# Full-height matrix products, no one-column products, and another placing of the preparation in a fused graph and state-space kernel

## The chip, the cores and the metric

The kernel runs on one core of a Trainium2 chip. The metric is the device time in microseconds of one execution. The engines are named as in the profile: PE (matrix products), DVE (vector), ACT (activations), POOL (GpSimd) and SP (which issues most DMAs).

## The reference

The input is x with shape (16, 96, 64, 64), float32. Two layers are computed. The first is a graph convolution on windows of 8x8 pixels; the second is a Mamba block with two inner layers on the sequence of 4096 pixels, followed by a fusion product and a batch norm. Cut to what matters:

```
# graph layer, per window of 64 nodes with 96 channels
y    = fc1(x)                                  # 1x1 convolution, scale, shift
xn   = nodes / max(norm(nodes), 1e-12)
idx  = top_k(-(sq - 2 xn xn^T + sq^T), 9)      # the 9 nearest nodes, itself among them
h    = gelu(ew [x_i ; x_j - x_i])              # 192 channels, for each neighbour j
x1   = fc2(max over j of h) + x
# Mamba block, twice, per sequence of 4096 pixels
h    = layernorm(seq) * ln_g + ln_b
xs,z = split(h @ in_w)                         # 192 channels each
xc   = silu(causal conv of 4 taps of xs)
dt,B,C = split(xc @ xproj_w)                   # 6, 16 and 16 columns
delta  = softplus(dt @ dt_w + dt_b)
s_t  = exp(delta A) s_(t-1) + delta B xc       # 192 channels x 16 states
y    = sum over states of s C + D xc
seq += (y * silu(z)) @ out_w
# end
out  = batchnorm(fus_w [seq ; relu(mean(x1) @ gp_w^T)]) + x1
```

## The kernel before

The sequence of an image is cut into 8 chunks of 512 pixels (one row of windows each). An item n = (b, i, k) is chunk k of inner layer i of image b; there are 16x2x8 = 256 items. An item has 8 slots p, one for each pair of the 16 states, so the main loop (L741) has 2048 slots. Channels and the two states of a pair lie on the 128 partitions, as three blocks c of 512 columns.

A slot does the following. DVE makes two products db (L648) of u = delta xc with bt and then three scans (L789); the first db of the next slot comes between the second and the third scan. bt is the row of B broadcast to the partitions by a PE product with the selecting matrix bsel (L643); it has one PSUM buffer, so PE makes the next bt when DVE has made the last db of the present one, and DVE needs it ahead of its third scan. ACT computes the decays da (L637) two slots ahead (`AHEAD`). POOL multiplies the states hb with the broadcast C, ct (L803). PE folds the two halves of the product of the slot before into ya and yb (L659, L661), and at p = 3 adds D xc with a diagonal matrix (L656, L657). At p = 1 of the next item DVE gates y with z (L667).

All other work is written as Python generators. In each slot, ahead of the second scan (`c == 1`), every generator in the list `going` is advanced by one step up to its next `yield`. So the order on each engine is written out by hand: a step's instructions stand in each engine's queue between those of the slot. The main ones, with the slot in which each starts:

- `norm` (L509), started at p = 7 for item n+3: the centred product pc (L520), its square on ACT (L522), and the sum over channels by `by_pixel` (L271): four products whose weights are 96x128 pieces of the square and whose moving operand is the one column ones_c, giving the variances as 128x4. DVE scales them (L527), POOL takes the power -0.5 (L530), and two DMAs through DRAM spread it over the 96 partitions (rs, L533 and L535). POOL makes hn (L538).
- `prelude` (L540), started at p = 5 for item n+2 at the head of the list: the convolution and z products (L555, L560) with SiLU on ACT (L567), the product pd (L579), its copy dbl (L584), the products pdta and pdtb (L593, L596) and the softplus as four ACT passes (L600 to L607), four POOL passes (L609 to L613), and 12 DMAs that arrange delta and u.
- `nearest` (L288) and `edges` (L360), one row of windows in two items: fc1, norms of the nodes (again by `by_pixel`, ss, with POOL powers and DMAs), similarities sc, top 8 on DVE; then one-hots on ACT (L384, L385), products pv, gathered products t (L404, L407) with GELU on ACT (L412), maxima over the neighbours on DVE (L793, one after each scan, out of the queue `between`), the maximum against the own node sa (L455), and the product pf with fc2 (L462, L465), added to x on DVE (L474).
- `tail` (L670), started at p = 4: the product with out_w, added to seq on DVE (L686), and in the second inner layer the fusion product po (L693), o on ACT (L695) and statistics on DVE (L697).

Two mechanisms matter. Products of steps use the PSUM pool `ps_m` (pm) in turn, which has two buffers: a product waits until the one two before it has been read. And `apart` splits a step: its product is made at the end of the present slot's steps, and DVE's use of it stands at the head of the next slot's. ACT's exponential and SiLU or GELU lie in different tables; a step that yields `TABLE` keeps `ahead` from running in the next slot, so that the table changes once.

The products of bt, pdta and pdtb contract over 39 rows (6 + 32 columns of pd and a row of ones), those of the convolution and z over 97 (96 channels and a row of ones).

Before the loop, the first image's 8 rows of windows and the first items are prepared by `drain`; behind it the batch norm streams all outputs from DRAM.

```
    for m, (n, p) in enumerate(order):
        ...
        if p == 7 and n + 3 < NI:
            going.insert(0, norm(n + 3))
        if p == 5 and n + 2 < NI:
            going.insert(0, prelude(n + 2))
        ct, das = soon.pop((n, p))
        dbs = [first, times_b(n, p, 1, bt), times_b(n, p, 2, bt)]
        if after is not None:
            bt = bcast(*after)
        if p == 0 and behind is not None:
            folded(*behind, y)
```

## Time and profile before

| | |
|---|---|
| median of 3 runs | 14862.89 us (14855.65 to 14863.29) |
| profiled execution, its own time | 14897.12 us |
| its span | 14895.3 us |
| mean granted TensorE clock | 0.891 |
| PE busy | 13574.3 us (91%) |
| DVE busy | 13114.8 us (88%) |
| ACT busy | 10114.4 us (68%) |
| POOL busy | 10278.8 us (69%) |
| scans L789, with carried state | 5376 of 1269 ns mean |
| db L648 | 6144 of 680 ns mean |
| POOL hb L803 | 2048 of 3450 ns mean |
| ACT da L637 | 6144 of 710 ns mean |

The mean of an instruction includes its start and end phases, which overlap with its neighbours'; where times are added up along an engine, the distance from start to start is the right measure (1.19 us for a scan, 0.59 us for a db in DVE's timeline). A float32 product has two records on PE for each instruction. An engine's busy share is a mean over the whole span; which engine a slot waits for is read from the waits and from windows of the timeline.

### The profile page before, as it was taken

What the parts mean: (1) busy time and instruction counts of PE and PEld (TensorE: products, weight loads), DVE (VectorE), ACT (ScalarE), POOL (GpSimd) and SP (SyncE); (2) the same over time, 40 slices, a digit from 0 to 9 for tenths busy, and PEclk for the clock granted to TensorE, in tenths of its full rate; (3) what the DMA queues carried; (4) which work ended last, traced back from release to release, by engine and by line L of the source; (5) the groups of instructions that cost most, each with busy time, mean ns of one, the idle gap of its engine ahead of it and who ended that gap; (6) DMA issues with size and microseconds to landing.
All of it is one profiled execution on the core that took longest, in us unless ns stands there. A gap on an engine that the chain in (4) does not pass through costs nothing. (4 is left out here: it accounts for less than half of the span.)

```text
span 14895.3 us, 168323 instructions
## 1 busy us (share of the span) xinstructions
PE 13574.3 (91%) x50248; PEld 5491.6 (37%) x50248; DVE 13114.8 (88%) x17401; ACT 10114.4 (68%) x14517; POOL 10278.8 (69%) x6279
## 2 busy tenths in 40 slices
PE   5799999999999999999999999999999999999982
PEld 2233333333333333333333333333333333333330
DVE  2699999999998999999999999999999999999984
ACT  4477777777777777777777777777777677677652
POOL 0577777777777777777777777777777777777771
PEclk8799899989998999999999999999999999989885
DMA  1233333333333333333333333333333333333337
GB/s 27 61 82 86 83 82 83 84 83 81 86 84 79 85 84 83 80 85 85 81 84 84 83 81 86 84 80 85 83 83 82 84 86 80 85 83 82 81 81 218
DMA packets 934023, 1256.95 MB, mean 84 GB/s; under 512 B 304672, under 2 KB 436142, under 8 KB 923888
## 3 DMA queue, kind: packets, MB, share of 16 engines
q1 hardware_dynamic: 929520, 1221.01, 31.7%
q10 hardware_dynamic: 3584, 25.17, 0.4%
q8 instruction: 396, 6.49, 0.2%
q14 instruction: 523, 4.28, 0.1%
HBM read 756.89 MB, written 85.98 MB: 57 GB/s over the span
## 5 line engine op out<-in xcount | busy, mean ns | idle before, releaser
L803 POOL TENSOR_TENSOR hb<-hb,ct 128x1536 f32<-128x1536 f32 x2048 | 7065.1, 3450 | 678.1 <-DVE hb L789 187.2
L789 DVE TENSOR_TENSOR_SCAN hb<-da,state,db 128x512 f32<-128x512 f32 x5376 | 6781.1, 1269 | 0.0
L648 DVE TENSOR_TENSOR db<-u,bt 128x512 f32<-128x512 f32 x6144 | 3992.1, 680 | 672.4 <-PE bt L643 670.3
L637 ACT ACTIVATE da<-delta,a 128x512 f32<-128x512 f32 x6144 | 3900.5, 710 | 61.6 <-DVE hb L789 48.6
L643 PE MATMUL bt<-dbl,bsel 39*128 39x512 f32 x4096 | 2466.0, 683 | 333.6 <-DVE db L648 330.3
L659 PE MATMUL ya<-hb,fold 128*64 128x512 f32 x8192 | 2424.8, 673 | 89.4 <-POOL hb L803 89.1
L802 POOL COPY state<-hb 128x3 f32<-128x3 f32 x1792 | 337.8, 189 | 2975.2 <-DVE hb L789 2550.8
L412 ACT ACTIVATE g<-t,eb,es 128x512 f32<-128x512 f32 x1536 | 1184.8, 777 | 1015.8 <-PE t L404 728.1
L567 ACT ACTIVATE xc<-pj,conv_b 128x512 f32<-128x512 f32 (+1 forms) x512 | 297.4, 581 | 1959.6 <-PE pj L555 1018.8
L661 PE MATMUL yb<-hb,fold 128*64 128x256 f32 x8192 | 1368.8, 415 | 0.0
L404 PE MATMUL t<-oh,vu 128*128 128x512 f32 x2048 | 1176.1, 700 | 45.7 <-ACT vu L393 29.4
L661 PEld LDWEIGHTS yb<-hb,fold 128*64 128x64 f32 x8192 | 640.5, 150 | 1359.0 <-issue 1358.7
L643 PEld LDWEIGHTS bt<-dbl,bsel 39*128 39x128 f32 x4096 | 659.4, 201 | 1164.1 <-DVE db L648 634.7
L555 PE MATMUL pj<-hn,conv_in 97*128 97x512 f32 x2048 | 953.0, 608 | 27.9 <-POOL hn L538 27.9
L789 DVE TENSOR_TENSOR_SCAN hb<-da,db 128x512 f32<-128x512 f32 x768 | 922.6, 1209 | 0.0
L659 PEld LDWEIGHTS ya<-hb,fold 128*64 128x64 f32 x8192 | 503.6, 145 | 1070.4 <-issue 726.9
L407 PE MATMUL t<-oh,vu 128*64 128x512 f32 x2048 | 583.7, 649 | 214.2 <-ACT g L412 209.2
L584 ACT COPY dbl<-pd 38x512 f32<-38x512 f32 x256 | 148.3, 579 | 855.9 <-PE pd L581 855.9
L404 PEld LDWEIGHTS t<-oh,vu 128*128 128x128 f32 x2048 | 386.2, 211 | 801.4 <-issue 521.4
L793 DVE TENSOR_REDUCE hqa<-g 128x64 f32<-128x512 f32 x960 | 634.1, 661 | 0.4 <-ACT g L412 0.3
L390 PE MATMUL pv<-ewT,y 96*64 96x192 f32 x2048 | 478.1, 361 | 124.7 <-ACT sqv L522 124.4
L384 ACT ACTIVATE oh<-idb,minus_node 64x1024 f32<-64x1024 uint16 x512 | 586.9, 1146 | 6.7 <-DMA idb<-idxd 6.7
(160 smaller groups left out, 18671.8 us busy)
## 6 DMA issues: line engine op xcount, KB each, us to landing
ct<-cd SPq DMA_DIRECT2D x4096, 128.0 KB, 3.0
delta<-ln SPq DMA_DIRECT2D x1024, 128.0 KB, 2.4
u<-s SPq DMA_DIRECT2D x1024, 128.0 KB, 2.3
idb<-idxd SPq DMA_DIRECT2D x256, 256.0 KB, 4.0
delta<-ln SPq DMA_DIRECT2D x1024, 64.0 KB, 2.0
u<-s SPq DMA_DIRECT2D x1024, 64.0 KB, 2.0
rs<-rsd SPq DMA_DIRECT2D x256, 192.0 KB, 3.4
x<-in_x SPq DMA_DIRECT2D x128, 192.0 KB, 4.5
```

What stands on the lines that cost most here:

```text
L384: nc.scalar.activation(ohj, idb[:, 2 * p : 2 * p + 2, :], AF.Abs, bias=minus_node)
L404: nc.tensor.matmul(t, lhsT=vus[p][:, part, :128], rhs=ohw[part], start=True, stop=True)
L412: nc.scalar.activation(g, t, AF.Gelu, bias=e_b[:, j : j + 1], scale=e_s[:, j : j + 1])
L555: nc.tensor.matmul(ps, lhsT=wt[:, t, :128], rhs=hn[:, off : off + Q], start=(t == 0), stop=(t == taps - 1))
L637: nc.scalar.activation(da, delta[:, c, :], AF.Exp, scale=a_neg[i][:, c, p : p + 1])
L643: nc.tensor.matmul(bt, lhsT=bsel[:, p, :], rhs=made[n][2], start=True, stop=True)
L648: nc.vector.tensor_tensor(db, made[n][5][:, c, :], bt, ALU.mult)
L659: nc.tensor.matmul(y[0][half(h)], lhsT=fold, rhs=hb[:, h, :], start=(p == 0), stop=(p == NPR - 1))
L661: nc.tensor.matmul(y[1][half(h)], lhsT=fold, rhs=hb[:, 2, bass.ts(h, QH)], start=(p == 0), stop=(p == NPR - 1))
L789: nc.vector.tensor_tensor_scan(hb[:, c, :], das[c], dbs[c], state[:, p, c : c + 1] if k else 0.0, ALU.mult, ALU.add)
L793: between.popleft()()
L803: nc.gpsimd.tensor_tensor(hb, hb, ct.unsqueeze(1).to_broadcast([128, NB3, Q]), ALU.mult)
```

## The change

It has these parts.

- The one-column products go. The sums over channels are made by one product with a 96x96 matrix of ones (ones_cc), which gives the sum on all 96 partitions at once. For `norm` ACT takes Ln and Exp(-0.5 ·) of it, and the DVE and POOL steps and both DMAs go. For `nearest` ACT copies one row, which two DMAs through DRAM arrange as 128x4; the clamp moves to POOL.
- bsel, hn, dbl, z_in, conv_in and dt_w get 128 rows; the added weight rows are zero and the added rows of hn and dbl are ones.
- `norm` starts at p = 0 for item n+2, `prelude` at p = 4 at the end of the list, with one `yield` fewer ahead of pd and one more ahead of the exponentials; `tail` starts at p = 6, `pooled` at k = 5.
- The one-hots of both halves are made in one step, right after the wait for their indices, instead of in the steps of pv.
- The maxima over neighbours are queued a slot later (`later` has two stages), and the maximum against sa goes after the second scan of its slot (`late`).
- The decays are computed ahead at p = 2 and 4 (`BURSTS`) and at the end of the slots.
- D xc is added at p = 0 instead of p = 3. z has four buffers, o shares the buffer of xn, and hqa and hqb are allocated later.

```diff
-    bsel = const.tile([R + 2 * NS + 1, NPR, 128], F32, name="bsel")
+    bsel = const.tile([128, NPR, 128], F32, name="bsel")
...
-        t = const.tile([R + 2 * NS + 1, Q], F32, name=f"dbl{i}")
+        t = const.tile([128, Q], F32, name=f"dbl{i}")
...
-            wc = const.tile([C + 1, NT, D], F32, name=f"conv_in{i}")
+            wc = const.tile([128, NT, D], F32, name=f"conv_in{i}")
+            nc.vector.memset(wc, 0.0)
...
+        ss = pm.tile([C, Q], F32, tag="mm", name=f"ss_{nm}")
+        nc.tensor.matmul(ss, lhsT=ones_cc, rhs=sq, start=True, stop=True)
+        nc.scalar.copy(sq[0:1], ss[0:1])
+        ss_d = dram.tile([1, Q], F32, tag="ss_d", name=f"ssd_{nm}")
+        nc.sync.dma_start(out=ss_d, in_=sq[0:1])
         r4 = pr.tile([128, 2, QJ], F32, tag="r4", name=f"r4_{nm}")
-        apart(partial(by_pixel, sq, f"ss_{nm}"), clamped)
+        nc.sync.dma_start(out=r4[:, 1], in_=ss_d.rearrange("o (p j) -> (o p) j", j=QJ))
+        yield
+        yield
+        nc.gpsimd.tensor_scalar(r4[:, 0], r4[:, 1], 1e-24, None, ALU.max)
...
             yield
+            for p in range(2):
+                ohj = ohs[p][0:NN].rearrange("j w i k -> j w (i k)")
+                nc.scalar.activation(ohj, idb[:, 2 * p : 2 * p + 2, :], AF.Abs, bias=minus_node)
+                nc.scalar.activation(ohj, ohj, AF.Relu, bias=1.0, scale=-1.0)
             yield
...
-                    later.append(
+                    later[1].append(
...
+        late.append(partial(nc.vector.tensor_tensor, hqa, hqa, sa, ALU.max))
+        late.append(partial(nc.vector.tensor_tensor, hqb, hqb, sb, ALU.max))
...
-        v4 = pr.tile([128, QJ], F32, tag="v4", name=f"v4_{nm}")
-        apart(
-            partial(by_pixel, sq, f"pvar_{nm}"),
-            lambda ps: nc.vector.tensor_scalar(v4, ps, 1.0 / C, EPS, ALU.mult, ALU.add),
-        )
-        yield
-        nc.gpsimd.tensor_tensor(v4, v4, mhalf, ALU.pow)
-        yield
-        rs_d = dram.tile([128, QJ], F32, tag="rs_d", name=f"rsd_{nm}")
-        nc.sync.dma_start(out=rs_d, in_=v4)
+        ps = pm.tile([C, Q], F32, tag="mm", name=f"pvar_{nm}")
+        nc.tensor.matmul(ps, lhsT=ones_cc, rhs=sq, start=True, stop=True)
         rs = pr.tile([C, Q], F32, tag="rs", name=f"rs_{nm}")
-        nc.sync.dma_start(out=rs, in_=rs_d.rearrange("p j -> (p j)").unsqueeze(0).to_broadcast([C, Q]))
-        yield
+        nc.scalar.activation(rs, ps, AF.Ln, bias=eps_t[:C], scale=1.0 / C)
+        nc.scalar.activation(rs, rs, AF.Exp, scale=-0.5)
         yield
...
-        if p == 7 and n + 3 < NI:
-            going.insert(0, norm(n + 3))
-        if p == 5 and n + 2 < NI:
-            going.insert(0, prelude(n + 2))
+        if p == 0 and n + 2 < NI:
+            going.insert(0, norm(n + 2))
+        if p == 4 and n + 2 < NI:
+            going.append(prelude(n + 2))
...
-                if p == 4 and n:
+                if p == 6 and n:
                     going.append(tail(n - 1))
                 open_steps()
-                if not held:
+                if p in BURSTS:
                     ahead()
...
+            while c == 1 and late:
+                late.pop(0)()
```

## Prediction

> **What bounds the kernel now.** I read the page first, then the waits, the stretches by window and the timeline of one period. The page:

> ```profile
> span 14895.3 us, 168323 instructions
> PE 13574.3 (91%) x50248; PEld 5491.6 (37%) x50248; DVE 13114.8 (88%) x17401; ACT 10114.4 (68%) x14517; POOL 10278.8 (69%) x6279
> ...
> PEclk8799899989998999999999999999999999989885
> ```

> PE and DVE are both near full, and PE's granted clock is mostly nine tenths of full. The waits (in total, times, longest):

> ```profile
> DVE db L648 <- PE bt L643: 670.3, 546, 12.3
> ...
> DVE x L474 <- PE pf L465: 314.0, 83, 5.2
> ```

> DVE's idle time is mostly a wait for PE: for the broadcast product bt, of which there is one buffer, and for pf. From the starts of the first scan of each slot I get the frame: the slots run from 497 us to 14,614 us; 121 periods of two items (16 slots) take 110.9 us each, of which DVE works 101.7 and is idle 9.2; the last 7 periods, without graph work, average about 101. Ahead lie 497 us, behind 281 us of batch norm.

> Where the idle time sits is told by the clock. Five windows (length, then busy time of PE, PEld, DVE, ACT, POOL; the last three columns are granted clock, DMA share, GB/s), then PE's and DVE's timeline there:

> ```profile
> 6040.60:6044.00 3.40, 3.40 (x13) 1.79 (x12) 3.16 (x6) 3.39 (x6) 2.31 (x2) 1.00 0.12 28
> 6044.00:6047.40 3.40, 2.50 (x12) 2.34 (x10) 3.15 (x4) 3.29 (x7) 2.48 (x2) 0.50 0.45 60
> 6047.40:6050.80 3.40, 3.40 (x10) 1.27 (x10) 1.42 (x3) 3.35 (x6) 3.00 (x2) 0.50 0.22 49
> 6050.80:6054.20 3.40, 2.53 (x6) 0.60 (x4) 2.56 (x4) 2.00 (x2) 3.19 (x5) 0.99 0.00 0
> 6054.20:6057.60 3.40, 2.53 (x14) 0.77 (x12) 3.40 (x5) 1.70 (x3) 3.32 (x3) 1.00 0.04 1
> ```
> ```profile
> 6039.58 2.03 PE L275 MATMUL pvar<-ones_c,sqv 96*128 96x1 f32 x8
> 6041.54 1.12 PE L643 MATMUL bt<-dbl,bsel 39*128 39x512 f32 x2
> 6042.51 1.02 PE L593 MATMUL pdta<-dbl,dt_w 39*128 39x512 f32 x2
> 6043.45 0.65 PE L596 MATMUL pdtb<-dbl,dt_w 39*64 39x256 f32 x4
> ...
> 6045.48 2.00 PE L275 MATMUL ss<-ones_c,sq 96*128 96x1 f32 x8
> 6047.40 1.98 PE L659 MATMUL ya<-hb,fold 128*64 128x512 f32 x4
> ```
> ```profile
> 6051.64 0.70 DVE L648 TENSOR_TENSOR db<-u,bt 128x512 f32<-128x512 f32 x1 [2.71 <-PE bt L643]
> ```

> PE was busy for all of the first window, with one-column products and 39-row products, and its clock was halved at the end of it. In the fourth it was busy for 2.53 of 3.40 us, mostly with 128-row products, and kept the full clock. At half clock the fold (ya) takes 1.98 us where it takes 1.03 elsewhere; bt comes late and DVE stands still for 2.71 us. Over 1000 to 14,400 us the clock records hold 330 such stretches, 2526 us in all, about one per item; 651 us of DVE's 1118 us idle lie in them.

> [...] most half-clock stretches last 3.4, 6.8 or 10.2 us. [...] I counted each window's streaming time weighted by rows/128 (a half-width product counts half): a limit of 0.35 of the window sorts 98% of the full-clock windows into those that keep the clock and those that lose it; from half clock the limit is 0.71 of the time, the same work. Hence a 39-row bt counts 0.3 of a 128-row one. [...] so the zero rows should cost nothing (here L656 on 128 rows has 0.43 us per pass back to back, L593 on 39 rows also 0.43). [...]

> **The change part by part** (start-to-start times at full clock from the trace; a period is two items, "even" is the one with ss and pf2).
> - *pvar and ss.* Removed per item: 4 one-column products, 1.96 us on PE (6039.58 to 6041.54), one DVE eviction (0.08 us of DVE's time), one POOL power of 1.02 us and two DMAs; per even item the same for ss, 2.0 us and two evictions. Added: one 96x512 product each, 0.95 us (L520 pc), two ACT passes for pvar (0.48 each as L522), one ACT copy for ss, and two DMAs on SP with a wait for the copy. Over the run PE loses 256x1.0 + 128x1.05 = 390 us, POOL 260 us, DVE 0.3 us a period; ACT gains 512x0.48 + 128x0.48 = 307 us. ACT is at 68%, so its total is hidden; its order is not (below). The ss path waits for two DMA trips, about 2 x 2.4 us by the page's issue rows, against two slots (12 us) until the power: hidden; queued behind them on SP are ct loads, needed two slots later: nothing.
> - *128 rows* (bt, pdta, pdtb; the 97-row convolutions): time nothing, bounds -0.1 to +0.1 us per slot, since bt to the next start is 1.05 us and 0.86 would be two bare passes. Activity: bt alone adds 0.86x0.7 = 0.6 us of the 1.19 us that a window needs.
> - *Clock.* With pvar at full width and wide rows, every slot I add up is over the limit except the stretch below. If no half clock is left, 651 us of DVE's idle go, 5 us a period.
> - *Moves.* Sums per slot of PE against DVE, layer-1 items. Before, slots 7 and 0 together held 12.9 and 14.3 us of PE against 12.6 and 12.2 of DVE. After: 9.8 and 9.5 against 11.3 and 12.2. The convolution moves to slots 4 and 5 (6.0 and 5.7 against 7.1 and 7.1), the reductions move with it, one-hots (4 us of ACT) to slots 5/6, where ACT is two slots ahead: nothing. The preparation's POOL passes (L609 to L613, 7.1 us) go from slots 2 and 3 to 1 and 2, and meet hn (1.25 us) there: POOL has 15.4 us in these two slots against 12.9 of DVE, 2.5 us of lag that slot 3 (3.6 us) takes up and three hb buffers bridge; the twelve delta and u DMAs and cd go out a slot earlier, so SP's later ct loads stand behind them as before. The late max against sa moves between the scans of slot 6; its 2.3 us of DVE stay. The whole period: PE 90.9, DVE 101.4, ACT 79, POOL 78. So DVE is the bound.
> - *What is late next: slots 0 and 1 of even items.* Count from the end of slot 7's last scan. POOL's product of that slot ends at 3.6, the fold at 5.0, pc at 5.95, pv at 6.6, bt(2) at 7.65, pvar at 8.6. ACT has sqv at its head, which waits for pc: 6.45; behind it e, s1, ln, s1 (3.4 us) to 9.8, vu to 10.2, three da to 12.0, and only then the Ln of pvar, 12.5, its Exp and the copy of ss, 13.5. The product pool has two buffers: ss waits for vu (10.2 to 11.15), po for the Ln (12.5 to 13.4), pf2 for the copy (13.5 to 15.3), dp and fold to 18.05, bt(3) to 19.1. DVE wants pf2 at 14.0 and bt(3) at 17.7: it waits 1.3 + 1.4 = 2.7 us. Without po (layer 0) 0.2 + 1.5 = 1.7. Mean 2.2 per period. In odd items bt(3) comes in time.
> - *Half clock there.* From 8.6 to 12.5 PE streams only ss, 0.64 us by weight: a window starting in about 2.2 of its 3.4 us of phase falls under 1.19 us. Then pf2, fold and bt take 1.7 to 2.6 us longer. 0.6 x 2.1 = 1.3 us per period.
> - *Rest:* 1.0 us per period, half of the 1.9 (227 us in 121 periods) that DVE now waits for bt at full clock.

> The sum: idle 2.2 + 1.3 + 1.0 = 4.5 us per period. 121 x (101.4 + 4.5) = 12,814; the last 7 periods 7 x 91 = 637 (their DVE work, 101.4 less about 12.5 of graph work, and 2 idle); 497 + 10 ahead (a norm moves into the loop, ss has one more DMA trip per row); 281 behind. Together 14,239 us against the span of 14,895. The profiled execution took 14,897, 34 us more than the median of the runs; taking 34 off gives 14,205, I say 14,200 us, 4.5% faster.

> **Rivals.**
> - *A: DVE's floor.* If ACT gets to the Ln earlier than I think, and no half clock is left, idle is 1 us: 121 x 102.4 + 637 + 788 - 34 = 13,780. For it: PE has 10 us spare per period. Against: the two buffers and ACT's order stand in the program.
> - *B: the half clock stays in slots 0 and 1 of both items,* because zero weights or the rows don't count, or PE idles more since DVE bounds. Idle 7.5: 121 x 108.9 + 637 + 788 - 34 = 14,570. The change would then not do what its first words say, but the one-column products are gone. Against: the count by rows above.
> - *C: slower.* ACT[...] holds sqv, then the Ln behind the exponentials; PE waits for it in slot 1 of each item, bt with it, and the idle window halves the clock over the fold as now. It decides from 9.5 us idle per period (now 9.2, DVE 0.3 less), that is 4.8 us per item where I have 2.7 at worst plus 2.6. At 10.5: 121 x 111.9 + 637 + 788 - 34 = 14,930. Against: odd items show 4 us of room.

> **How the numbers follow.** Forecast (idle 3 to 6 us, 14,020 to 14,390) 0.45; A (below that) 0.22; B (to 14,750) 0.26; C 0.05; within 0.2%, about what a measurement of this kernel tells from no change, 0.02. Faster 0.93, same 0.02, slower 0.05. The range leaves out the lower half of A and the upper half of B: 13,870 to 14,560.

> **What would show it.** Right: granted clock over 0.95, DVE's share over 93% of the loop, the wait of db for bt under 350 us, the Ln of pvar about 4 us after its product in even items, PE's busy share falling to some 85%. Wrong: clock still at 0.9 with bt on 128 rows (rows don't count); DVE waits in slots 2 to 5 for g or xc (ACT's order, not slot 1); longer passes of bt (then zero rows cost time).

## The result and the profile after

The changed kernel takes 14,749.7 us (median of 4 runs, 14,746.09 to 14,751.98) where the kernel before took 14,863.1 in the same series: a ratio of 0.9925, 95% interval 0.991 to 0.9941. It is 0.75% faster; I had said 4.5%. The page of the profile after:

```profile
span 14744.3 us, 163116 instructions
PE 12702.7 (86%) x47944; PEld 4800.3 (33%) x47944; DVE 12880.3 (87%) x16893; ACT 10542.4 (72%) x15157; POOL 10059.0 (68%) x6151
...
PEclk7899999999999999999999999999999999999985
```

PE lost 872 us of busy time, as planned, and DVE 234. But DVE's share is 87% where it was 88%: it is not kept busy any better. The mean granted clock rose from 0.891 to 0.928. The waits (in total, times, longest):

```profile
DVE db L637 <- PE bt L632: 897.3, 448, 47.8
...
PE bt L632 <- DVE db L637: 442.8, 472, 5.3
...
DVE x L471 <- PE pf L462: 432.1, 126, 4.7
...
PE t L403 <- ACT g L408: 267.7, 124, 4.5
...
PE ss L306 <- ACT vu L382: 228.7, 119, 1.9
PE pf L290 <- ACT rl L589: 225.9, 120, 1.9
```

DVE waits longer for bt (before 670.3) and for pf (before 314.0), though PE has much less to do. And PE waits itself: for DVE's last db ahead of bt, and for ACT ahead of t, ss and pf.

In the frame of the prediction (periods of two items, counted from the starts of the scans; means over the 4th to the 110th) a period took 110.87 us before and takes 109.62 now. DVE's work in it fell from 101.70 to 99.77, and its idle time rose from 9.17 to 9.84. The loop is 152 us shorter: 234 us less work, 82 us more idle. So in DVE's account the 0.75% is cheaper work, and the better clock brought it no less idle time. An account tells no cause: runs e1 and e2 below test the cheaper work, e3, e4 and e6 the clock.

By slot, DVE's idle time per period was before 2.49 (slot 0 of even items), 2.94 (slot 2), 1.18 (slot 0 of odd items), 0.82 (slot 3 of odd items) and the rest small. After it is 1.77, 5.03, 0.07 and 2.84. Half clock holds 20.46 us of a period before and 12.08 after; of DVE's idle time, 4.59 us lay in it before and 5.64 after (at full clock 4.58 and 4.20). There is less half clock, but more of DVE's idle time lies in it.

One stretch of an odd item, with a wait longer than most, shows how. Windows of PE's clock after (length, then busy time of PE, PEld, DVE, ACT, POOL; then granted clock, DMA share, GB/s), cut where the clock changes:

```profile
6037.30:6040.70 3.40, 1.39 (x8) 0.36 (x8) 3.40 (x5) 3.37 (x7) 3.07 (x2) 1.00 0.29 80
6040.70:6044.10 3.40, 3.18 (x4) 1.17 (x4) 3.40 (x5) 3.40 (x6) 3.32 (x3) 0.50 0.00 0
6044.10:6047.50 3.40, 1.51 (x3) 0.30 (x2) 3.40 (x5) 2.18 (x3) 3.40 (x3) 0.99 0.00 0
6047.50:6050.90 3.40, 2.54 (x6) 0.77 (x8) 1.03 (x1) 1.29 (x2) 3.24 (x4) 0.51 0.41 96
6050.90:6054.30 3.40, 3.40 (x10) 1.31 (x7) 0.00 (x0) 0.40 (x2) 2.52 (x1) 0.50 0.59 143
```

PE's timeline there (start, duration, instruction; in brackets the idle time ahead of it and what ended it):

```profile
6040.92 2.07 PE L632 MATMUL bt<-dbl,bsel 128*128 128x512 f32 x2 [2.23 <-DVE db L637]
...
6046.36 1.13 PE L400 MATMUL t<-oh,vu 128*128 128x512 f32 x2 [1.88 <-ACT g L408]
6048.36 1.98 PE L403 MATMUL t<-oh,vu 128*64 128x512 f32 x4 [0.87 <-ACT g L408]
6050.12 1.92 PE L648 MATMUL ya<-hb,fold 128*64 128x512 f32 x4
6051.83 1.07 PE L650 MATMUL yb<-hb,fold 128*64 128x256 f32 x4
6052.82 1.88 PE L632 MATMUL bt<-dbl,bsel 128*128 128x512 f32 x2
```

and DVE's:

```profile
6054.74 0.70 DVE L637 TENSOR_TENSOR db<-u,bt 128x512 f32<-128x512 f32 x1 [6.21 <-PE bt L632]
```

In the first window DVE and ACT work without a pause, and PE is done early: it has nothing to do for 2.23 us until DVE has made the last db of the slot. It was busy for 1.39 of 3.40 us, and the clock is halved. In the third window it waits 1.88 us for ACT's GELU, ahead of which ACT made six decays and loaded a table (1.28 us), and the clock is halved again, now over t, the folds and the next bt. They take 1.98 us (L403), 1.92, 1.07 and 1.88 where at full clock, from 6106.76 us on, the same lines take 1.08, 1.03, 0.60 and 1.12, and DVE stands still for 6.21 us. At full clock the same four steps take some 3.5 us from start to start instead of 6.4, so by this estimate the clock makes about 2.9 us of that wait; the rest is PE's late start.

Counted over the 4th to the 110th period, the clock was lost 2.64 times a period before. In 1.88 of them PE had no pause over 0.05 us in the window ahead, as in the first window that the prediction shows; in most of the others, 0.64, it waited for DVE's db. After, it is lost 2.73 times, and PE waits in every one of these windows: the longest wait is for ACT in 2.33 of them and for DVE's db in 0.40. Its busy share in the window ahead was 100% at the median before and is 35% after.

DVE's cheaper work is mostly one instruction, the maximum against sa. Before (timeline of DVE and POOL), then after:

```profile
6018.67 3.44 POOL L803 TENSOR_TENSOR hb<-hb,ct 128x1536 f32<-128x1536 f32 x1
...
6020.62 2.04 DVE L455 TENSOR_TENSOR hqa<-hqa,sa 128x512 f32<-128x512 f32 x1
```
```profile
L785 DVE TENSOR_TENSOR hqa<-hqa,sa x120: 658/664/668, 811.0 to 13853.9; 128x512 f32<-128x512 f32 x120
```

The second fence has the shortest, median and longest duration in ns. Before, the median was 2037 ns: the maximum starts while POOL's product runs, and ends 0.55 us after that product's end (6018.67 + 3.44 = 6022.11; 6020.62 + 2.04 = 6022.66). So it is for all 120 of these maxima in the loop of the kernel before, within 0.02 us, whether the maximum starts 1.86 or 2.16 us into the product. The eight ahead of the loop, where no such product runs, take 0.68 us. In its new place it starts 0.08 to 0.40 us after POOL's product is over, and takes 664 ns. From start to start this is 1.33 of the 1.93 us that DVE's work lost per period. The rest is the evictions of pvar and ss (0.30) and small parts, among them the second half of the gate of y (0.16). The scans are not held up: in the kernel before they take 1.27 us at the median beside POOL's work and without it. Why the one waits and the others don't, no run shows.

### The profile page after: what moved, and what is told of

Read it like the earlier page. It is cut to its first block, busy times and chain, and to the rows that moved or that the text cites. A ratio compares the mean times of both kernels' runs of the same rounds, so it can differ in the third digit from the quotient of the medians.

```text
span 14744.3 us, 163116 instructions
## 1 busy us (share of the span) xinstructions
PE 12702.7 (86%) x47944; PEld 4800.3 (33%) x47944; DVE 12880.3 (87%) x16893; ACT 10542.4 (72%) x15157; POOL 10059.0 (68%) x6151
## 5 line engine op out<-in xcount | busy, mean ns | idle before, releaser
L632 PE MATMUL bt<-dbl,bsel 128*128 128x512 f32 x4096 | 2376.3, 663 | 448.1 <-DVE db L637 442.8
L648 PE MATMUL ya<-hb,fold 128*64 128x512 f32 x8192 | 2325.7, 648 | 196.9 <-POOL hb L795 189.7
L650 PE MATMUL yb<-hb,fold 128*64 128x256 f32 x8192 | 1305.3, 398 | 0.0
L400 PE MATMUL t<-oh,vu 128*128 128x512 f32 x2048 | 1061.8, 643 | 58.8 <-ACT g L408 46.2
L632 PEld LDWEIGHTS bt<-dbl,bsel 128*128 128x128 f32 x4096 | 632.2, 194 | 1312.4 <-DVE db L637 802.3
L544 PE MATMUL pj<-hn,conv_in 128*128 128x512 f32 x2048 | 927.2, 595 | 9.1 <-POOL hn L527 9.1
L648 PEld LDWEIGHTS ya<-hb,fold 128*64 128x64 f32 x8192 | 515.5, 143 | 1141.3 <-issue 459.8
L403 PE MATMUL t<-oh,vu 128*64 128x512 f32 x2048 | 593.1, 659 | 271.6 <-ACT g L408 267.7
L598 POOL TENSOR_TENSOR e<-e,s 128x768 f32<-128x768 f32 x256 | 465.0, 1816 | 347.7 <-ACT s L596 347.7
L519 ACT ACTIVATE sqv<-pc 96x512 f32<-96x512 f32 x256 | 151.8, 593 | 701.2 <-PE pc L517 701.2
L400 PEld LDWEIGHTS t<-oh,vu 128*128 128x128 f32 x2048 | 419.4, 207 | 623.4 <-issue 454.4
```

What stands on the lines that cost most here:

```text
L400: nc.tensor.matmul(t, lhsT=vus[p][:, part, :128], rhs=ohw[part], start=True, stop=True)
L403: nc.tensor.matmul(t[half(h)], lhsT=vus[p][:, h, 128:], rhs=ohw[h], start=True, stop=True)
L544: nc.tensor.matmul(ps, lhsT=wt[:, t, :128], rhs=hn[:, off : off + Q], start=(t == 0), stop=(t == taps - 1))
L632: nc.tensor.matmul(bt, lhsT=bsel[:, p, :], rhs=made[n][2], start=True, stop=True)
L648: nc.tensor.matmul(y[0][half(h)], lhsT=fold, rhs=hb[:, h, :], start=False, stop=(p == NPR - 1))
L650: nc.tensor.matmul(y[1][half(h)], lhsT=fold, rhs=hb[:, 2, bass.ts(h, QH)], start=False, stop=(p == NPR - 1))
```

## The experiments

The theory after the result: the clock follows the work that PE does in a window, weighted by rows, as the prediction has it; but PE now waits for DVE and ACT, these waits fill windows, and the half clock moves to where bt and pf become late. It has three rivals: the clock is only a symptom, and DVE's idle time comes from the order on ACT, with the norm's step at the head of the list of steps; the rows don't count; and the moved maximum alone made the gain, as so much less work on DVE. The table has all runs. The ratio is that to the kernel before, run on the same chip in the same series; the per-period figures are sums over the trace, in us, as means over the 4th to the 110th period. The fences of every run are of its own profiled execution.

| kernel | median us | ratio (95%) | period | DVE work | DVE idle | of it at half clock | half clock |
|---|---|---|---|---|---|---|---|
| before | 14,863 | | 110.87 | 101.70 | 9.17 | 4.59 | 20.46 |
| after | 14,750 | 0.9925 (0.991 to 0.9941) | 109.62 | 99.77 | 9.84 | 5.64 | 12.08 |
| e1 | 14,601 | 0.9822 (0.9806 to 0.9839) | 108.33 | 100.46 | 7.88 | 4.40 | 8.11 |
| e2 | 14,985 | 1.0074 (1.0057 to 1.0091) | 111.68 | 100.62 | 11.05 | 6.11 | 22.82 |
| e3 | 14,967 | 1.0079 (1.0063 to 1.0096) | 111.34 | 99.84 | 11.50 | 7.02 | 15.61 |
| e4 | 14,246 | 0.9582 (0.9566 to 0.9598) | 105.41 | 99.78 | 5.63 | 0.51 | 1.00 |
| e5 | 14,017 | 0.9428 (0.9412 to 0.9444) | 103.68 | 99.60 | 4.08 | 1.54 | 6.49 |
| e6 | 14,754 | 0.9932 (0.9912 to 0.9953) | 110.15 | 101.67 | 8.48 | 4.54 | 12.69 |
| e7 | 15,326 | 1.0324 (1.0307 to 1.0341) | 114.72 | 101.4 | 13.34 | 7.39 | 23.11 |
| e8 | 13,818 | 0.9307 (0.9291 to 0.9322) | 102.00 | 99.6 | 2.38 | 0.01 | 1.32 |
| e9 | 13,870 | 0.9318 (0.9303 to 0.9334) | 102.44 | 100.3 | 2.15 | 0.67 | 2.99 |
| e11 | 13,829 | 0.9292 (0.9277 to 0.9308) | 102.07 | 100.3 | 1.76 | 0.00 | 1.29 |
| e12 | 13,764 | 0.9248 (0.9233 to 0.9264) | 101.53 | 99.6 | 1.95 | 0.00 | 0.00 |

**e1: the maximum back in its step** (the kernel after, with nothing else changed).

```diff
-        late.append(partial(nc.vector.tensor_tensor, hqa, hqa, sa, ALU.max))
-        late.append(partial(nc.vector.tensor_tensor, hqb, hqb, sb, ALU.max))
+        nc.vector.tensor_tensor(hqa, hqa, sa, ALU.max)
+        nc.vector.tensor_tensor(hqb, hqb, sb, ALU.max)
```

> The changed kernel with the maximum against sa put back ahead of the second scan, where the kernel before has it; all else stays. Theory P (the gain is mostly DVE's: in the kernel before this maximum takes 2.04 us because POOL's product of the states runs beside it, in the changed one 0.66): it takes 2 us again, DVE's work per period goes from 99.8 to about 101.1 us and the time to 14,850 to 14,920, so that all of the gain is gone. Theory C (the gain comes from the fewer half-clock stretches, 20.5 to 12.1 us a period): at most 40 us slower, since DVE waits for PE anyway. My forecast's step 'its 2.3 us of DVE stay' expects no change.

Measured: DVE's maximum costs 1.35 instead of 0.58 us per period, as it should; yet the kernel is faster by 1.0% of the time before (0.9822 against 0.9925). DVE's idle time in slot 0 of even items is gone (1.77 to 0), and so is every loss of the clock that began in slot 7 of odd items or in slot 0 (0.26 and 0.47 per period before the edit). DVE waits for bt 330 times instead of 448, 249 us less in all:

```profile
DVE db L637 <- PE bt L632: 648.6, 330, 45.8
```

A dearer instruction on the engine that bounds made the kernel faster. The theory that each microsecond saved on DVE is a gain falls (P in the text above). The other, C, allowed for no change but not for a gain, so neither foresaw this.

**e2: the late maximum alone,** in the kernel before.

```diff
+    late = []
...
-        nc.vector.tensor_tensor(hqa, hqa, sa, ALU.max)
-        nc.vector.tensor_tensor(hqb, hqb, sb, ALU.max)
+        late.append(partial(nc.vector.tensor_tensor, hqa, hqa, sa, ALU.max))
+        late.append(partial(nc.vector.tensor_tensor, hqb, hqb, sb, ALU.max))
...
+            while c == 1 and late:
+                late.pop(0)()
```

> The kernel before with one part of the change alone: the maximum against sa stands after the second scan. Theory P: the maximum takes 0.7 to 1.0 us, DVE's work per period falls by 1.0 to 1.3 us in slot 6 of odd items, where DVE does not wait for PE, so 100 to 160 us faster: 14,700 to 14,760, as fast as the whole change. Theory C: no change, 14,860.

Measured: 0.74% slower. DVE's work falls by 1.1 us per period (the maximum from 1.91 to 0.74), its idle time rises by 1.9, and half clock from 20.5 to 22.8. Neither theory foresaw this either. It is e1 the other way round; that DVE is sooner ready for bt and pf while PE is not sooner with them, and that the additional half clock costs the rest, is only argued here.

**e3: 39 and 97 rows in the kernel after** (bt, pdta, pdtb with 39, convolution and z with 97).

```diff
+    KD = R + 2 * NS + 1
...
-        nc.tensor.matmul(bt, lhsT=bsel[:, p, :], rhs=made[n][2], start=True, stop=True)
+        nc.tensor.matmul(bt, lhsT=bsel[:KD, p, :], rhs=made[n][2][:KD], start=True, stop=True)
```

It tests whether the clock goes by rows, as the count in the prediction has it: what follows if it does stands first, and then what follows if it doesn't.

> The changed kernel with bt, pdta and pdtb on 39 rows and the convolution and z products on 97 again, everything else as in the changed kernel. [...] bt counts 0.3 of a 128-row product, more windows fall under the limit, half-clock time rises from 12.1 us a period to 16 to 22, onsets appear in slots 0, 2 and 8 too, and the time rises by 50 to 250 us, to 14,800 to 15,000. If rows do not count: half-clock time 11 to 13 us and 14,750 within 30 us. If zero rows cost time: bt is shorter than 1.05 us from start to next start and the kernel faster.

**e6: 128 rows alone,** in the kernel before (bsel, hn, dbl and the weights get 128 rows as in the change; nothing else).

```diff
-    bsel = const.tile([R + 2 * NS + 1, NPR, 128], F32, name="bsel")
+    bsel = const.tile([128, NPR, 128], F32, name="bsel")
...
-        t = const.tile([R + 2 * NS + 1, Q], F32, name=f"dbl{i}")
+        t = const.tile([128, Q], F32, name=f"dbl{i}")
```

> The kernel before with the 128 rows alone (one-column products, order and placing stay). If rows count: the half-clock stretches that start in slots 1 and 9 still start (pvar and ss fill two thirds of those windows with one-column products) but end sooner, half-clock time falls from 20.5 to 10 to 16 us a period, DVE's idle from 9.2 by 1 to 3 us: 14,500 to 14,740. If rows do not count: 14,860.

Measured: without the rows the kernel after is 1.5% slower (1.0079 against 0.9925), with half clock at 15.6 instead of 12.1 us and a mean granted clock of 0.910 instead of 0.928. With the rows alone the kernel before is 0.7% faster, half clock falls from 20.5 to 12.7, and the granted clock is 0.927 instead of 0.891. So rows count for the clock here. Zero rows cost bt no time, as its lines show, of e6 and then of the kernel before (shortest, median, longest, in ns):

```profile
L645 PE MATMUL bt<-dbl,bsel x4096: 592/677/1223, 492.0 to 14476.6; 128*128 128x512 f32 x196
```
```profile
L643 PE MATMUL bt<-dbl,bsel x4096: 589/693/1219, 493.0 to 14606.2; 39*128 39x512 f32 x196
```

The shortest differ by 3 ns. In e6, too, the wait moves on: DVE's idle time in slot 0 of even items falls from 2.49 to 0.39, and that in slot 3 of odd items rises from 0.82 to 3.01, where PE waits 3.60 us for ACT's GELU instead of 1.60. The time, 14,754 us, is just above the 14,500 to 14,740 that I had expected.

**e4: PE kept at work** (the kernel after, with 13 products of zero weights per period, 256 columns each, that leave the result as it is).

```diff
+    zeros = const.tile([128, 1], F32, name="zeros")
+    nc.vector.memset(zeros, 0.0)
...
+    def idle(count, alone=False):
+        if y is not None:
+            for _ in range(count):
+                nc.tensor.matmul(y[1], lhsT=zeros.to_broadcast([128, 128]), rhs=conv_in[0][:, 0:2, :128], start=alone, stop=alone)
...
+        idle(3)
         pf = pm.tile([C, Q], F32, tag="mm", name=f"pf_{nm}")
...
+        idle(3, True)
         ss = pm.tile([C, Q], F32, tag="mm", name=f"ss_{nm}")
         nc.tensor.matmul(ss, lhsT=ones_cc, rhs=sq, start=True, stop=True)
+        idle(2, True)
...
+                    if hf == 1 and p == 0 and part == 2:
+                        idle(2)
...
+            if p == 1 and n % 2:
+                idle(3)
```

> The changed kernel with added products whose weights are all zero and whose result is not used (or adds zero), at the places where PE waits: 3 ahead of fc1's product, 3 ahead of ss and 2 behind it, 3 at the end of slot 1 and 2 between the gathered products of slot 2 in odd items; each 128x256 columns, 0.43 us at full clock, 5.6 us a period. If the half clock is what makes bt late (the clock as cause): half-clock time falls from 12.1 us a period to under 3, DVE's idle in slots 1 to 3 of odd items (2.8 us) and in slot 0 (1.8) goes, and in spite of 5.6 us more PE work the time falls by 200 to 500 us, to 14,250 to 14,550. If PE's waits for ACT are the cause and the half clock only goes with them: no gain, or 100 to 400 us slower.

Measured: 3.4% of the time before faster than the kernel after, 500 us, with more work on PE and nothing else changed. The waits:

```profile
DVE db L651 <- PE bt L646: 619.2, 449, 47.9
...
DVE x L485 <- PE pf L476: 208.3, 126, 3.5
```

DVE waits for the same two products, as often as before the edit, but less long. The mean granted clock rises from 0.928 to 0.972, half clock falls from 12.08 to 1.00 us per period, and of DVE's idle time the part at half clock from 5.64 to 0.51, while the part at full clock does not fall (4.20 and 5.12). By themselves the added products only delay what stands behind them on PE (POOL's hb waits for them 30 times, 73.2 us in all). So the clock is a cause and not only a symptom, and it was worth 4.2 of the 9.8 us. It is not the whole cause everywhere. In slot 0 of even items DVE's idle time falls from 1.77 to 0.57 us and in slot 2 from 5.03 to 2.74, but in slot 3 of odd items, where I had expected it to go, only from 2.84 to 2.11: there PE still waits 1.95 us for ACT's GELU. The added work is 3168 records of PE, two for each product: 26 in a period, by an estimated 0.214 us each (half of the 0.43 us that 512 columns take) 5.6 us.

**e5: the norm's step at the end of the list.**

```diff
-            going.insert(0, norm(n + 2))
+            going.append(norm(n + 2))
```

> The changed kernel with the norm step put at the end of the list in place of its head. Then ACT has the exponentials and the copy vu ahead of the square that waits for pc, and PE has ss and po ahead of pvar. If ACT's order is what delays pf and bt in slots 1 and 2 of even items (5.0 us of DVE's 9.8 us idle per period): their idle falls to 1 to 2.5 us and the time by 300 to 480 us, to 14,270 to 14,450. If the half clock alone makes them late: the idle there stays above 4 us, time within 100 us of 14,750.

Measured: 5.0% of the time before faster than the kernel after, 732 us, by one line, and more than the 300 to 480 us expected. What it mends is seen in the kernel after, in slots 1 and 2 of an even item (timeline of PE, ACT and DVE):

```profile
6091.21 1.02 PE L522 MATMUL pvar<-sqv,ones_cc 96*96 96x512 f32 x2
...
6094.15 1.07 PE L306 MATMUL ss<-sq,ones_cc 96*96 96x512 f32 x2 [1.92 <-ACT vu L382]
...
6095.76 0.67 ACT L524 ACTIVATE rs<-pvar,eps_t 96x512 f32<-96x512 f32 x1
...
6096.48 2.02 PE L459 MATMUL pf<-hqa,fc2T 128*96 128x512 f32 x2 [1.26 <-ACT rs L524]
...
6100.25 0.75 DVE L471 SCALAR_TENSOR_TENSOR x<-pf,fc_b,x 96x512 f32<-96x512 f32 x1 [2.68 <-PE pf L462]
```

Here is the chain of the prediction: the Ln of pvar starts 4.5 us after its product does, ss and pf2 (the pf of fc2) wait for a buffer of the product pool, and in these waits (1.92 and 1.26 us) the clock is halved, from 6095.34 to 6102.16 us, so pf takes 2.02 us where fc1's takes 1.10 at full clock (L290, 6082.80), and DVE waits 2.68 us. With the norm at the end of the list the waits are these:

```profile
DVE db L637 <- PE bt L632: 600.1, 386, 45.8
...
DVE x L471 <- PE pf L462: 21.8, 8, 3.4
```

Of 126 waits for pf eight are left (432 us to 22), and DVE's idle time in slot 2 falls from 5.03 to 0.14. Slot 0 of even items (1.89) and slot 3 of odd ones (1.75) remain. So the order of the steps is a cause too. The line moves the norm's step in the queues of ACT and of PE at once (pvar now stands behind ss and po), and the run doesn't tell the two apart. Clock and order are both causes, and they overlap: slot 0 of even items is mended by e4 alone, slot 2 there by either, mostly by e5, and slot 3 of odd items in part by each.

**e7: the sums over channels at full width alone,** in the kernel before (39 rows stay, and so does every placing). The part for the norm is shown; that for ss is made in the same way.

```diff
-        apart(
-            partial(by_pixel, sq, f"pvar_{nm}"),
-            lambda ps: nc.vector.tensor_scalar(v4, ps, 1.0 / C, EPS, ALU.mult, ALU.add),
-        )
...
+        ps = pm.tile([C, Q], F32, tag="mm", name=f"pvar_{nm}")
+        nc.tensor.matmul(ps, lhsT=ones_cc, rhs=sq, start=True, stop=True)
         rs = pr.tile([C, Q], F32, tag="rs", name=f"rs_{nm}")
...
+        nc.scalar.activation(rs, ps, AF.Ln, bias=eps_t[:C], scale=1.0 / C)
+        nc.scalar.activation(rs, rs, AF.Exp, scale=-0.5)
```

> The kernel before with the full-width sums alone: pvar and ss as one 96x512 product each, with the Ln and Exp on ACT or the copied row and its two DMAs; 39 rows, order and placing stay. If one-column products are the main cause of the half clock in slots 1, 9 and 15: half-clock time falls from 20.5 to under 8 us a period, PE's work by 3 us, DVE's idle from 9.2 to 3 to 5 us: 14,200 to 14,500, better than the whole change. If PE's waits in the two-buffer pool come in their place: idle 7 to 10, 14,700 to 14,900.

Measured: 3.2% slower, though PE's one-column products are gone; I had expected a gain or no change. The waits:

```profile
DVE db L630 <- PE bt L625: 1137.7, 543, 54.7
...
ACT rs L514 <- PE pvar L512: 731.8, 254, 5.5
```

The Ln stands in ACT's queue right behind the step that makes its product, and ACT stands still there for 2.9 us each time; before, DVE took the variances in the next slot. And half clock rises from 20.5 to 23.1 us, with DVE's idle time at half clock up by 2.8 us and that at full clock by 1.4. The run doesn't separate ACT's wait from the clock. It shows that the full-width sums, by themselves and in the old places, are a loss.

**e8, e9, e11, e12: both cures together.** e8 is e5 with three of the five groups of zero-weight products:

```diff
-            going.insert(0, norm(n + 2))
+            going.append(norm(n + 2))
...
+        idle(3)
         pf = pm.tile([C, Q], F32, tag="mm", name=f"pf_{nm}")
...
+                    if hf == 1 and p == 0 and part == 2:
+                        idle(2)
...
+            if p == 1 and n % 2:
+                idle(3)
```

> The changed kernel with the norm step last (as e5) and zero-weight products at the two places where PE still waits there: 3 ahead of fc1's product in slot 7 of odd items, 3 at the end of slot 1 and 2 between the gathered products in slot 2 of odd items. If the half clock is the cause of the 4.1 us that DVE is still idle in e5 (slots 0 and 11): half-clock time from 6.5 to under 1 us a period, idle 1 to 2 us, 13,680 to 13,820. If it is PE's wait for the GELU results and for the softplus: idle stays at 3.5 to 4.5 and the time at 14,000 or above.

e9 is e5 with the edit of e1, and has no additional products:

```diff
-            going.insert(0, norm(n + 2))
+            going.append(norm(n + 2))
...
-        late.append(partial(nc.vector.tensor_tensor, hqa, hqa, sa, ALU.max))
-        late.append(partial(nc.vector.tensor_tensor, hqb, hqb, sb, ALU.max))
+        nc.vector.tensor_tensor(hqa, hqa, sa, ALU.max)
+        nc.vector.tensor_tensor(hqb, hqb, sb, ALU.max)
```

> The changed kernel with both orders altered and nothing added: the norm step last and the maximum against sa ahead of the second scan. If DVE's wait in slot 0 (1.9 us a period with the norm last) is made by the half clock that starts when PE runs ahead of DVE in slots 14 and 15: the slower maximum (about 0.7 us more work in slot 14) takes it away as it did in e1, idle falls from 4.1 to about 2.2 us, 13,840 to 13,920. If DVE's work is what counts: 0.7 us a period more, 14,090.

e11 is e9 with the last two groups of e8:

```diff
+                    if hf == 1 and p == 0 and part == 2:
+                        idle(2)
...
+            if p == 1 and n % 2:
+                idle(3)
```

> As e9, with zero-weight products only in odd items: 3 at the end of slot 1, 2 between the gathered products of slot 2. Of the idle that e9 leaves, slot 11's 1.75 us falls to 0.8 as in e8: 13,740 to 13,850. If the idle in slot 11 is PE's wait for GELU results and not the clock: as e9 or slower.

e12 is e8 with the products of slot 1 moved to where PE waits in it, ahead of pvar:

```diff
-            if p == 1 and n % 2:
-                idle(3)
...
+        if n % 2:
+            idle(3, True)
         ps = pm.tile([C, Q], F32, tag="mm", name=f"pvar_{nm}")
```

> As e8, with the 3 products of slot 1 of odd items moved from the end of the slot to the place ahead of pvar, where PE waits 1.6 us for the square anyway, so that they cost no PE time: DVE's idle in slot 10 (0.6 us) goes, half-clock time stays under 1.5 us a period: 13,720 to 13,800. If their place does not matter for the clock but the window after them does (slot 10 and 11): half clock comes back there and 13,850 to 14,000.

Measured: all four lie between 0.925 and 0.932, each in the range expected for its time, though e8 keeps 2.38 us of idle time where 1 to 2 were expected. Most of this comes from order alone: e9, with no added product, is 6.8% faster than the kernel before, and the products of e11 bring 0.3% more. Their place counts: e12 has as many as e8 and is faster by 0.6% of the time before, since DVE's idle time in slot 2 of odd items (0.62 in e8) is gone. The best, e12, takes 13,763.67 us, 7.5% less than the kernel before and 6.7% less than the kernel after. Its page:

```profile
span 13762.6 us, 167106 instructions
PE 12458.3 (91%) x49906; PEld 4950.1 (36%) x49906; DVE 12856.4 (93%) x16894; ACT 10520.3 (76%) x15157; POOL 10047.1 (73%) x6151
```

No half clock is left between the 4th and the 110th period. PE is busy for 244 us less than in the kernel after, though it does 8 products more per period; none of its products there runs at half clock. DVE's idle time is 1.95 us per period, and all else is its work, so this is near DVE's floor.

## Why the prediction was wrong

The sum has 14,239 us for the profiled execution's span, and it was 14,744: 505 us more. By terms, now over all 121 periods: DVE's work 99.6 instead of 101.4 us per period (-220 us), its idle time 10.0 instead of 4.5 (+663), the last seven periods 708 instead of 637 us (+71, as DVE is idle for 10.7 us in each of them where I had 2), ahead and behind -9.

- **The step that failed is "Clock":** "every slot I add up is over the limit except the stretch below". I added up PE's work over slots, most of them 5 to 7 us long, and over a slot it does suffice: recounted in the kernel after and weighted by rows, it is 0.46 to 0.92 of each slot, and 0.35 only in slot 1 of even items, the stretch that I had excepted. But the clock changes in steps of 3.4 us (between 1000 and 14,400 us every one of the 330 half-clock stretches before and the 339 after is one to four times that long), and work that suffices for a slot can lie in one half of it. It does so once PE is faster than DVE and ACT: then PE waits, 1.97 us a period for DVE's db ahead of bt in slot 2 of odd items, 2.16 us for the GELU in slot 3, 1.89 us for ACT's reading of the pool in slot 7. Before, PE had too little weight in a few windows but was busy in most of them; now it is idle in them. The half clock got less (20.5 to 12.1 us), but the idle time in it rose from 4.6 to 5.6 us instead of falling to the 1.3 of "Half clock there". e4 shows it: with only PE's waits filled, 5.1 of the 5.6 us go, and all idle time falls by 4.2. So this step makes about 2.9 of the 5.3 us that were missing in the term for idle time (4.2 less the 1.3; means over the 4th to the 110th period). The other 2.4 are left in e4: 5.63 where I had 2.2 + 1.0 without the clock.
- **The limit itself held.** As a count in the two traces it did: weighted by rows, 0.384 of a window sorts 99.9% of the full-clock windows of the kernel after into those that keep the clock and those that lose it (0.35 and 98% before). Nine in ten keep it in any case, so that is the share to beat; with the rows left out, the best limit sorts some 95% before. e3 and e6 show that rows count. With it I could have tested the new order window by window; I used it on one stretch alone.
- **"What is late next" was right in its chain, wrong in its reach.** The Ln of pvar comes 4.5 us after its product (I had said about 4), and ss and pf2 wait as described: with the half clock there I had 3.5 us for slots 0 to 2 of even items, and slot 2 alone took 5.0. Slot 0 took 1.8 more, 1.2 of it (by e4) from a clock that is lost from slot 7 on, which I had not seen. e5 shows that this chain is worth 5.0%, more than I thought; its half clock goes with it (12.1 to 6.5 us).
- **"In odd items bt(3) comes in time" was wrong:** 2.84 us in slot 3 of odd items. PE's wait for the GELU was not in the sum. The half clock of the timeline above is only a part of it: e4, with hardly any half clock, leaves 2.11, e5, with the order alone, 1.75, and e12, with both, 0.96. This slot is most of the 2.4 us that e4 leaves over.
- **"Its 2.3 us of DVE stay" was wrong to the good side:** the maximum against sa costs 1.33 us less in its new place, where POOL's product isn't running (0.66 instead of 2.04 us for its first part). The gain of DVE's work, 234 us, is more than the whole gain of the change. But e1 and e2 show that this is bookkeeping and no cause: the cheaper place of the maximum itself costs 1.0% in the kernel after and 0.7% in the one before.
- **"128 rows: time nothing" was right** (e6: 3 ns), and so was PE's busy share, 86% where I had said some 85%. The signs of the clock failed: it is 0.928 and not over 0.95, and the wait of db for bt is 897 us and not under 350.
- **One reading was off before the change.** By the same trace 557 of DVE's 1118 us of idle time lie in half clock, not 651: 4.6 us a period and not 5. This moves no other term of the sum.
- **The rivals.** The result lies at the upper end of B, the half clock that stays. One of its reasons holds, that PE idles more; the others do not, since the rows and the zero weights do count, and slot 3 of odd items was not among its slots. C had its deciding point at 9.5 us idle per period, and the 9.84 are beyond it: in the sum only DVE's cheaper work, which I had left out, makes up for it. A, DVE's floor, 13,780 us, is what e12 reaches by other means, 13,764.

The parts don't simply add up. The rows are worth 0.7% in the kernel before and 1.5% in the one after, and each edit moves PE's waits into other windows. In the kernel before, rows alone are -0.7%, full-width sums alone +3.2% and the late maximum alone +0.7%, while the whole change is -0.75%; the new placing of the steps, the decays and the one-hots was not run by itself, so what it gives alone stays open. Open, too, are why the clock's windows fall as they do in e1 and e2, and how much of e7 is ACT's wait. Not tried: a third buffer of the product pool, and da issued later than the Ln.

## What to carry to other kernels

When PE is made faster than the engines that feed it, sum its work over windows of the clock, not over loop steps, and look at where it will wait: here waits of 2.23 and 1.88 us in windows of 3.4 us were followed by half clock for the next products, and these were the ones that the bounding engine needed. If such waits can't be removed, a few products with zero weights in them can be cheap insurance (e4: 5.6 us of PE per period, by the estimate above, for 4.2 us of the whole). But look first at which step stands ahead of which in an engine's queue: one line that put the norm's step last was worth more than the whole rewrite (e5), and with two edits of the order and no added product (e9) the kernel is within 0.8% of the best run (e12).
